# A recommendation kernel with 1.1 million gathered rows: transposes in four PSUM banks, attention as columns, shrinking lags, and another split of the row queues

## The chip, the cores and the metric

The kernel runs on one core of a Trainium2 chip. The metric is the time of the device in microseconds (us), as the median of several runs; smaller is better. The core has five engines that work in parallel, each through its own queue in order: TensorE (PE, matmuls), VectorE (DVE), ScalarE (ACT), GpSimd (POOL) and SyncE (SP). GpSimd, ScalarE and SyncE can each issue DMAs.

## The reference

For each of 16,384 users there are 69 item ids and one label id. Each id picks a row of 96 floats from a table `emb` of 100,001 rows. What is computed, in float32:

```
u  = emb[batch_user]                    # 16384 x 69 x 96
ql = emb[batch_label]                   # 16384 x 96
z  = [ql, u, ql - u, ql * u]            # 384 wide
h  = dice(z @ W1 + b1)                  # 64 wide
att = (h @ W2 + b2) @ W3 + b3           # one number for each user and item
pre = u * att  where id < 100000, else 0
pooled = window @ pre                   # 69 items summed into 10 groups
x  = [pooled, ql]                       # 11 * 96 wide
x  = dice(x @ Wf1 + bf1); x = dice(x @ Wf2 + bf2)      # 200, then 80 wide
out = x @ Wf3 + bf3
dice(x) = (a * (1 - p) + p) * x,  p = sigmoid(x)
```

## The kernel before

The users are cut into 32 blocks of 512. Within a block the items are cut into 69 chunks of 512 rows: 64 chunks hold 8 users with their first 64 items each ("main"), 5 hold one of the last items of all 512 users ("tail"). A step `i` takes two chunks, so there are 1104 steps (`NPAIR`). A chunk is four tiles of 128 rows, one row per partition.

**Getting rows.** Most tiles are fetched by GpSimd with one indirect DMA of 128 rows (`gather`, L268) into a buffer `u` of the step; 17 such buffers take turns. One tile in some of the chunks (`SLOT`) is fetched otherwise: SyncE or ScalarE issues 128 DMAs of one row each (class `Singles`, L303) into one of the buffers of `ring`, four for SyncE and three for ScalarE. `SP_CHUNKS` and `ACT_CHUNKS` list these chunks. SyncE has a tile every 10 steps. ScalarE has a tile every 8 steps and issues 16 rows of it in each step, between its activations (`ACT_ROWS`). For each group of rows the offsets are loaded into registers first (L288).

**The work of a step**, in the order of the data:

- `fetch` (L361): TensorE transposes the eight tiles, four to a PSUM bank `ptr` (pool `ps_tr`, two banks); VectorE copies it to `uT` (L378) and multiplies it with the label's row to `quT` (L381).
- `hidden` (L391): TensorE makes the first layer of both chunks in one bank `ph` (L401, L405), ScalarE the sigmoid `y` (L407). `product` (L411): two VectorE operations make dice out of it.
- `attend_rows` (L417): for four steps together, TensorE makes the attention numbers as rows of a bank `prow` (L421), ScalarE copies them to `row` (L423). `turn_band` (L433): TensorE transposes `row` into `patt` (L438), so that the numbers stand one to a partition. `weigh` (L443): VectorE makes of `patt` the weights `rw` of the ten groups (L448).
- `pool_sums` (L460): eight matmuls of 20 columns of `u` with `rw` into a set of `acc` (three sets), `pool_copy` (L482): VectorE copies it to `pooled`. After `pool_sums` the buffer `u` is free for a gather 17 steps on.
- Tail chunks: `attend_tail` (L426) makes the attention over all partitions (`pa`) and VectorE the product `pre` (L431).
- For each block, once: `head_gather`, `head_turn` and `head_rows` prepare the label's rows, and `top1` to `top3` (L508 to L541) make the last three layers. The last block's top is made in four quarters of 128 users.

PSUM has eight banks here: two `ps_tr`, two `ps_h`, two `ps_x` (prow, patt, pa, pq, pc), one `acc`, one `ps_m` (the top).

**The order** is written out by hand: a dictionary `plan` gives each step its list of work, and every engine carries out its part in that order (`at`, L631). Lags keep the stages apart: in step `i` the transposes are those of `i`, `hidden` that of `i - 2`, `product` that of `i - 3`, `pool_sums` that of `i - 9` (`POOL_LAG`). Near the end, from step `c - 8` on with `c = NPAIR - 8`, another list is written out, with smaller lags. The last tail chunks of a block are its last five; in the last block they are moved forward (`EARLY`, `chunk_of`).

Of the kernel before, what the change touches and what calls it, by code (L numbers as in the profile page):

```python
# [18 lines left out]
P = 128  # L19
# [21 lines left out]
POOL_LAG = 9  # L41
# [5 lines left out]
CLOSE = 8  # L47

# [3 lines left out]
SP_CHUNKS = [2 * (10 * s + 8) + 1 for s in range(109)]  # L52
SP_RING = 4
ACT_CHUNKS = [2 * (8 * s + 11) for s in range(136)]
ACT_RING = 3
ACT_ROWS = 16
# [6 lines left out]

def chunk_of(c):

    n, k = divmod(c, NCH)
    if n == NBLK - 1 and k >= EARLY:
        k = NMAIN + k - EARLY if k < EARLY + NTAIL else k - NTAIL
    return n, k
# [47 lines left out]
def rec_kernel(  # L117
# [132 lines left out]
    ps_tr = ctx.enter_context(tc.tile_pool(name="ps_tr", bufs=2, space=PSUM))  # L250
    ps_h = ctx.enter_context(tc.tile_pool(name="ps_h", bufs=2, space=PSUM))
    ps_x = ctx.enter_context(tc.tile_pool(name="ps_x", bufs=2, space=PSUM))
    ps_acc = ctx.enter_context(tc.tile_pool(name="ps_acc", bufs=1, space=PSUM))
    acc = ps_acc.tile([E, 3, 2, NS, G], F32, tag="acc", name="acc")
    ps_m = ctx.enter_context(tc.tile_pool(name="ps_m", bufs=1, space=PSUM))


# [86 lines left out]
    def head_rows(n):  # L344

        for h in range(2):
            pc = ps_x.tile([P, NMAIN // 8, H1], F32, tag="x", name=f"pc{n}_{h}")
            for k in range(NMAIN // 8):
                x = (h * NMAIN // 8 + k) * 4 * NS
                nc.tensor.matmul(pc[E:P, k, :], qTs[n % 2][:, x : x + 4 * NS], Cq, start=True, stop=True)  # L350
            nc.scalar.copy(As[n % 2][E:P, h * NMAIN // 8 : (h + 1) * NMAIN // 8, :], pc[E:P])
# [65 lines left out]
    def attend_rows(b, n):  # L417

        pr = ps_x.tile([P, 512], F32, tag="x", name=f"prow{b}")[0 : 32 * n]
        for k in range(n):  # L420
            nc.tensor.matmul(pr[32 * k : 32 * (k + 1), :], v2, ys[b + k], start=True, stop=True)  # L421
        row = rpool.tile([P, 512], F32, tag="row", name=f"row{b}")[0 : 32 * n]
        nc.scalar.copy(row, pr)  # L423
        bands[b] = row
# [8 lines left out]
    def turn_band(b, n):  # L433

        row = bands.pop(b)
        pt = ps_x.tile([P, 4, n, 32], F32, tag="x", name=f"patt{b}")
        for t in range(4):
            nc.tensor.transpose(  # L438
                pt[:, t].rearrange("p k j -> p (k j)"), row[:, t * P : (t + 1) * P], ident[0 : 32 * n, 0 : 32 * n]
            )  # L440
        turned[b] = pt

    def weigh(b, n):  # L443

        pt = turned.pop(b)
        rw = rpool.tile([P, 16, 2, 2 * G], F32, tag="rw", name=f"rw{b}")[:, 0 : 4 * n]
        for j in range(2):
            nc.vector.scalar_tensor_tensor(  # L448
                rw[:, :, j, :],
                pt.rearrange("p t k j -> p (t k) j")[:, :, j : j + 1].to_broadcast([P, 4 * n, 2 * G]),  # L450
                bb,
                R.rearrange("p (o g) -> p o g", o=1).to_broadcast([P, 4 * n, 2 * G]),
                ALU.add,
                ALU.mult,
            )
        for k in range(n):
            rws[b + k] = rw[:, k::n]
            ys.pop(b + k)

    def pool_sums(i):  # L460

        u, rw = us.pop(i), rws.pop(i)
        todo = [(j, *chunk_of(2 * i + j)) for j in range(2)]
        todo = [(j, n, k) for j, n, k in todo if k < NMAIN]
        if not todo:
            return
        pa = acc[:, i % 3]
        for j, n, k in todo:
            for t in range(4):
                read_rows(  # L470
                    nc.tensor.matmul,
                    pa[:, j, 2 * t : 2 * t + 2, :].rearrange("e n g -> e (n g)"),
                    u,
                    2 * i + j,
                    t,
                    rw[:, t, j, :],
                    start=True,
                    stop=True,
                )
        accs[i] = pa, todo  # L480
# [27 lines left out]
    def top1(n, cols, h, part, p1):  # L508

        if part == 0:  # L510

            banks, tag = (ps_h, "h") if n == NBLK - 1 and cols.start >= BLK // 2 and h == 1 else (ps_m, "m")
            p1 = banks.tile([DH, BLK], F32, tag=tag, name=f"p1_{n}_{h}_{cols.start}")[:, cols]
# [13 lines left out]
    def top2(n, cols):  # L527
        x2 = xpool.tile([D2, BLK], F32, tag="x2", name=f"x2_{n}_{cols.start}")[:, cols]
        g2 = xpool.tile([DH, BLK], F32, tag="g1", name=f"g2_{n}_{cols.start}")[0:D2, cols]
        p2 = ps_m.tile([D2, BLK], F32, tag="m", name=f"p2_{n}_{cols.start}")[:, cols]  # L530
# [5 lines left out]
    def top3(n, cols, x2):  # L536
        k0, k1 = cols.start // P, cols.stop // P
        p3 = ps_m.tile([P, k1 - k0], F32, tag="m", name=f"p3_{n}_{cols.start}")
# [4 lines left out]
    def store(n):  # L543

        p4 = ps_x.tile([n, P], F32, tag="x", name="p4")
# [5 lines left out]
    def top3_last(x2):  # L551

        p3 = ps_m.tile([1, P], F32, tag="m", name="p3_last")
# [5 lines left out]
    pooled, pres, x1s, x2s, qs, us, hs, ys, bands, rws, p1s, gates, turned, accs = ({} for _ in range(14))  # L559

    def top_steps(n, cols):


        def half(h, part):
            if n not in x1s:
                x1s[n] = xpool.tile([DH, 2, BLK], F32, tag="x1", name=f"x1_{n}")
            p1s[n] = top1(n, cols, h, part, p1s.get(n))
# [9 lines left out]
    def rows_of(b, n):  # L577
        return lambda: attend_rows(b, n)

    def spread_of(b, n):  # L580
        def work():
            turn_band(b, n)
            weigh(b, n)

        return work
# [72 lines left out]
    e = c - CLOSE  # L658
    for i in range(e):
        if i >= 7 and i % 4 == 3 and i < e - 1:  # L660
            at(i, rows_of(i - 7, 4))
        if i >= 4:
            at(i, tails_of(i - 4))
        if i >= 8 and i % 4 == 0:
            at(i, lambda b=i - 8: turn_band(b, 4))
# [3 lines left out]
        pools = [] if i < POOL_LAG else [i - POOL_LAG]  # L669
        if i == e - 2:  # L670
            pools.append(i - POOL_LAG + 1)
        elif i == e - 1:
            pools = [i - POOL_LAG + 1]
        at(i, *[lambda k=k: pool_sums(k) for k in pools])
        if i >= 3:
            at(i, product_of(i - 3))
        at(i, *[lambda k=k: pool_copy(k) for k in ([] if i <= POOL_LAG else [i - POOL_LAG - 1, i - POOL_LAG][: 1 + (i == e - 1)])])
        if i == e - 2:
            at(i, rows_of(c - 16, 4))
        elif i == e - 1:  # L680
            at(i, lambda: turn_band(c - 16, 4))
        at(i, fetch_of(i))
        if i >= 8 and i % 4 == 0:
            at(i, lambda b=i - 8: weigh(b, 4))
        elif i == e - 1:
            at(i, lambda: weigh(c - 16, 4))

    at(e, product_of(e - 3), lambda: pool_copy(e - POOL_LAG), tails_of(e - 4))
    for i in range(e, c):
        if (i - 3) % 4 == 3:  # L690
            at(i, rows_of(i - 6, 4))
        at(i, tails_of(i - 3))
        if (i - 4) % 4 == 3:
            at(i, spread_of(i - 7, 4))
        at(i, hidden_of(i - 2), lambda i=i: scalar_rows(i))
        for k in {0: (-16, -15), 1: (-14,), 2: (-13,), 3: (-12, -11), 4: (-10, -9), 7: (-8, -7)}.get(i - e, ()):
            at(i, pool_of(c + k))
        at(i, fetch_of(i))

    at(c, pool_of(c - 6), pool_of(c - 5), tails_of(c - 3), hidden_of(c - 2), fetch_of(c))  # L700
    at(c + 1, tails_of(c - 2), hidden_of(c - 1), fetch_of(c + 1))
    at(c + 2, rows_of(c - 4, 4), tails_of(c - 1), hidden_of(c), spread_of(c - 4, 4), pool_of(c - 4), fetch_of(c + 2))
    at(c + 3, pool_of(c - 3), pool_of(c - 2), hidden_of(c + 1), fetch_of(c + 3, [hidden_of(c + 2)]))
    at(c + 4, pool_of(c - 1), fetch_of(c + 4, [hidden_of(c + 3)]))
    at(c + 5, rows_of(c, 4), spread_of(c, 4), pool_of(c), fetch_of(c + 5, [hidden_of(c + 4)]))
    at(c + 6, pool_of(c + 1), pool_of(c + 2), fetch_of(c + 6, [hidden_of(c + 5)]))
    at(c + 7, pool_of(c + 3), rows_of(c + 4, 2), fetch_of(c + 7, [spread_of(c + 4, 2), hidden_of(c + 6)]))

    for n in range(NBLK):
        first, end = n * NCH // 2, ((n + 1) * NCH - 1) // 2  # L710
        if n > 0:
            if n % NIDS == 1:
                at(max(0, first - 50), lambda n=n: load_ids(n))
            at(first - 14, lambda n=n: qs.__setitem__(n, head_gather(n)))
            at(first - 11, lambda n=n: head_turn(n, qs.pop(n)))
            at(first - 9, lambda n=n: head_rows(n))
        if n < NBLK - 2:
            for s, work in enumerate(top_steps(n, slice(0, BLK))):
                at(end + POOL_LAG + 4 + s, work)
        elif n == NBLK - 2:  # L720
            for s, work in enumerate(top_steps(n, slice(0, BLK))):
                at(end + POOL_LAG + 1 + s // 2, work)
# [3 lines left out]
    quarter = [top_steps(NBLK - 1, slice(r * P, (r + 1) * P)) for r in range(NQ)]  # L726
    for s, step in enumerate([1, 1, 1, 2, 2, 2, 2, 3, 3, 3]):
        at(c - 8 + step, quarter[0][s])
    for s, step in enumerate([5, 5, 5, 5, 6, 6, 6, 6, 7, 9]):
        at(c - 8 + step, quarter[1][s])  # L730

    d = NPAIR
    at(d, pool_of(c + 4), hidden_of(c + 7), pool_of(c + 5), *quarter[2][0:4], rows_of(c + 6, 2), quarter[2][4])
    at(d, spread_of(c + 6, 2), *quarter[2][5:8], pool_of(c + 6), quarter[2][8], pool_of(c + 7))
    at(d, quarter[2][9], quarter[3][0], lambda: store(B // P - 1), *quarter[3][1:])
# [79 lines left out]
```

## Time and profile before

| | |
|---|---|
| median of 3 runs | 10,930.59 us (10,930.19 to 10,933.84) |
| profiled execution, its own time | 13,684.32 us |
| its span, first to last instruction | 13,682.6 us |
| mean granted TensorE clock | 0.72 |
| busy: TensorE, VectorE, ScalarE, GpSimd | 9,106, 5,075, 991, 8,225 us |
| gathers by GpSimd | 8,587 of items, 128 of labels |
| row DMAs by SyncE, ScalarE | 13,952, 17,408 |

The profile is of one execution, and that one took a quarter longer than the runs. A row of its groups names a line of the kernel, the engine, what is written and read, the count, the busy time in us, the mean of one in ns, and the idle time of that engine just before, with what ended most of it. A matmul in float32 has two records, a transpose one. DMAs of single rows are not counted as busy.

### The profile page before, as it was taken

What the parts mean: (1) busy time and instruction counts of PE and PEld (TensorE: products, weight loads), DVE (VectorE), ACT (ScalarE), POOL (GpSimd) and SP (SyncE); (2) the same over time, 40 slices, a digit from 0 to 9 for tenths busy, and PEclk for the clock granted to TensorE, in tenths of its full rate; (3) what the DMA queues carried; (4) which work ended last, traced back from release to release, by engine and by line L of the source; (5) the groups of instructions that cost most, each with busy time, mean ns of one, the idle gap of its engine ahead of it and who ended that gap; (6) DMA issues with size and microseconds to landing.
All of it is one profiled execution on the core that took longest, in us unless ns stands there. A gap on an engine that the chain in (4) does not pass through costs nothing.

```text
span 13682.6 us, 171148 instructions
## 1 busy us (share of the span) xinstructions
PE 9106.3 (67%) x41797; PEld 4711.6 (34%) x41797; DVE 5074.9 (37%) x8639; ACT 990.6 (7%) x1657; POOL 8225.3 (60%) x8721
## 2 busy tenths in 40 slices
PE   3666666666666666666776666666666666676668
PEld 1333333333333333333333333333333333333334
DVE  2333333333333333333333333333333333333333
ACT  0000000000000000000000000000000000000001
POOL 5666566656666656666665665665665666556663
PEclk7677776777767777677776777777777777777677
DMA  1111111111111111111111111111111111111111
GB/s 38 34 34 33 34 33 33 33 35 33 33 34 34 35 33 33 33 33 36 33 33 33 33 36 33 34 33 33 36 33 33 34 33 35 33 33 34 33 33 22
DMA packets 344459, 458.45 MB, mean 34 GB/s; under 512 B 202354, under 2 KB 202866, under 8 KB 343330
## 3 DMA queue, kind: packets, MB, share of 16 engines
q0 software_dynamic: 278880, 428.92, 15.0%
q1 hardware_dynamic: 29762, 11.82, 0.4%
q10 hardware_dynamic: 34816, 6.75, 0.3%
q8 instruction: 336, 5.51, 0.2%
q14 instruction: 665, 5.45, 0.1%
HBM read 446.74 MB, written 0.07 MB: 33 GB/s over the span
## 4 chain that ended last, share of the span: by engine, by line
PE 37%; issue 20%; another core or an unknown queue 18%; ACTq 12%; DVE 10%; POOL 2%; ACT 1%; DMA 0%; POOLq 0%
ACTq L303 10%; PE acc L327 8%; PE ph L401 6%; PE ptr L327 6%; PE ph L405 5%; PE p L521 5%; DVE uT L378 3%; DVE quT L381 2%; POOL u L268 2%; PE prow L421 2%; DVE y L415 1%; DVE y L414 1%; ACTq L288 1%; PE pa L430 1%
## 5 line engine op out<-in xcount | busy, mean ns | idle before, releaser
L268 POOL DMA_INDIRECT u<-in_rows,ids x8587 | 8103.5, 944 | 5290.9 <-issue 2228.3
L327 PE MATMUL acc<-rw,u 128*96 128x20 f32 x15930 | 1972.9, 269 | 1685.7 <-issue 1088.5
L489 DVE COPY pooled<-acc 96x160 f32<-96x160 f32 x1008 | 429.0, 426 | 6575.4 <-remote 4728.2
L327 PEld LDWEIGHTS acc<-rw,u 128*96 128x96 f32 x15930 | 1853.6, 201 | 2757.0 <-issue 1954.3
L327 PE MATMUL ptr<-ident,u 128*96 128x128 f32 x8587 | 1655.6, 341 | 866.1 <-issue 659.3
L378 DVE COPY uT<-ptr 96x512 f32<-96x512 f32 x2208 | 1485.9, 673 | 996.2 <-remote 756.4
L405 PE MATMUL ph<-quT,wn 96*64 96x512 f32 x4416 | 1625.1, 727 | 195.2 <-issue 189.6
L401 PE MATMUL ph<-uT,A 128*64 128x512 f32 x4096 | 1637.7, 830 | 156.9 <-issue 106.2
L327 PEld LDWEIGHTS ptr<-ident,u 128*96 128x96 f32 x8587 | 1250.6, 166 | 1082.2 <-issue 864.1
L381 DVE TENSOR_TENSOR quT<-ptr,qT 96x512 f32<-96x512 f32 x2048 | 1378.6, 673 | 0.0
L407 ACT ACTIVATE y<-ph 128x512 f32<-128x512 f32 x1104 | 658.6, 597 | 8853.1 <-remote 3304.5
L405 PEld LDWEIGHTS ph<-quT,wn 96*64 96x64 f32 x4416 | 447.3, 175 | 1257.0 <-issue 1255.2
L414 DVE SCALAR_TENSOR_TENSOR y<-y,na1c,ph 128x512 f32<-128x512 f32 x1104 | 810.3, 734 | 177.1 <-ACT y L407 97.0
L415 DVE SCALAR_TENSOR_TENSOR y<-ph,wn,y 128x512 f32<-128x512 f32 x1104 | 828.8, 751 | 39.4
L521 PE MATMUL p<-pooled,wf 96*100 96x512 f32 (+1 forms) x1400 | 713.8, 643 | 84.9 <-issue 82.0
L438 PE MATMUL patt<-ident,row 128*128 128x128 f32 x1108 | 259.5, 375 | 641.4 <-issue 274.9
L421 PE MATMUL prow<-y,v 128*32 128x512 f32 x2208 | 540.7, 851 | 115.0 <-issue 95.6
L401 PEld LDWEIGHTS ph<-uT,A 128*64 128x64 f32 x4096 | 279.0, 169 | 868.9 <-issue 783.3
L521 PE MATMUL p<-pre,V 96*100 96x512 f32 (+1 forms) x700 | 424.0, 745 | 140.4 <-issue 89.2
L438 PEld LDWEIGHTS patt<-ident,row 128*128 128x128 f32 x1108 | 185.1, 194 | 775.8 <-issue 554.0
L521 PEld LDWEIGHTS p<-pooled,wf 96*100 96x100 f32 x1400 | 251.0, 192 | 450.3 <-issue 450.0
L430 PE MATMUL pa<-y,vrep 64*96 64x512 f32 x320 | 231.3, 895 | 203.2 <-DVE pre L431 127.6
(72 smaller groups left out, 2682.1 us busy)
## 6 DMA issues: line engine op xcount, KB each, us to landing
ring<-in_rows ACTq DMA_DIRECT2D x17408, 0.4 KB
ring<-in_rows SPq DMA_DIRECT2D x13952, 0.4 KB
u<-in_rows,ids POOLq DMA_INDIRECT x8587
ids<-in_idx SPq DMA_DIRECT2D x8, 560.0 KB, 2.5
q<-in_emb,ids POOLq DMA_INDIRECT x128
wf<-in_far SPq DMA_DIRECT2D x1, 1209.0 KB
wn<-in_near SPq DMA_DIRECT2D x1, 236.0 KB, 3.1
ids<-in_idx SPq DMA_DIRECT2D x1, 140.0 KB
```

What stands on the lines that cost most here:

```text
L268: nc.gpsimd.indirect_dma_start(out=dst, out_offset=None, in_=table, in_offset=bass.IndirectOffsetOnAxis(ap=index, axis=0),)
L303: d = self.engine.dma_start(out=ring[r : r + 1, b], in_=row_bytes[:, bass.ds(self.values[r], ROW_BYTES)]).then_inc(self.sems[k], 16)
L327: ins = op(out, ring[:, at[0]].bitcast(F32) if at else u[:, 4 * (c % 2) + t, :], other, **how)
L378: nc.vector.tensor_copy(uT[j][0:E], ptr)
L381: nc.vector.tensor_tensor(quT[:, j, :].rearrange("e (s f) -> e s f", f=FM), ptr.rearrange("e (s f) -> e s f", f=FM), by_field(q[:, k * NS ...
L401: nc.tensor.matmul(p, As[n % 2][:, k // 4, :], uT[j], start=True, stop=False)
L405: nc.tensor.matmul(p, Wp, quT[:, j, :], start=False, stop=True)
L407: nc.scalar.activation(y, ph, AF.Sigmoid, scale=S_DICE)
L414: nc.vector.scalar_tensor_tensor(y, y, na1c, ph, ALU.mult, ALU.mult)
L415: nc.vector.scalar_tensor_tensor(y, ph, a1c, y, ALU.mult, ALU.add)
L421: nc.tensor.matmul(pr[32 * k : 32 * (k + 1), :], v2, ys[b + k], start=True, stop=True)
L521: nc.tensor.matmul(p1, w[:, h * DH : (h + 1) * DH], x, start=(k == 0), stop=(k == KTOP - 1))
```

## The change

- **PSUM.** `ps_tr` has four banks, `ps_x` one. `ps_m` is gone: the top uses `ps_x`, and `ps_tr` for the last block's second half. One bank `shared` holds two sets of sums (columns 0 to 319), five places for attention numbers (320 to 479) and the last layer (from 480).
- **Attention as columns.** `attend_rows` and `turn_band` are gone. `attend` makes four matmuls per step with a 128 x 128 part of `y` as the loaded operand and two columns of `v2` as the moving one, so that the numbers come out one to a partition, in their place of `shared`; `weigh` reads them there.
- **Row queues.** SyncE has 136 tiles, one every 8 steps, ScalarE 98, one every 11 steps, with 12 rows per step. These are 234 tiles instead of 245; the rest stays with GpSimd.
- **Order.** `POOL_LAG` is 10; over the last 48 steps the lag of `pool_sums` goes down to 7 step by step, and attention bands go from four steps to two. In the last 12 and the last 8 steps the lags are smaller still. The quarters of the last block's top have a table `QUARTERS`. In the other blocks the tail chunks are spread (`TAIL_AT`: chunks 48, 53, 58, 63, 68), `head_rows` is made in two parts, and the steps of the top come at `end + 12` to `end + 20`.

```diff
-POOL_LAG = 9
+POOL_LAG = 10
...
+QUARTERS = [
+    [-12, -12, -11, -11, -10, -10, -9, -9, -8, -7],
+    [-5, -5, -5, -4, -3, -3, -3, -2, -1, 0],
+    [3, 3, 3, 4, 5, 5, 5, 6, 7],
+]
...
-SP_CHUNKS = [2 * (10 * s + 8) + 1 for s in range(109)]
+SP_CHUNKS = [2 * (8 * s + 8) + 1 for s in range(136)]
...
-ACT_CHUNKS = [2 * (8 * s + 11) for s in range(136)]
+ACT_CHUNKS = [2 * (11 * s + 14) for s in range(98)]
...
-ACT_ROWS = 16
+ACT_ROWS = 12
...
+TAIL_AT = [48 + 5 * f for f in range(NTAIL)]
...
-    ps_tr = ctx.enter_context(tc.tile_pool(name="ps_tr", bufs=2, space=PSUM))
+    ps_tr = ctx.enter_context(tc.tile_pool(name="ps_tr", bufs=4, space=PSUM))
...
-    ps_x = ctx.enter_context(tc.tile_pool(name="ps_x", bufs=2, space=PSUM))
+    ps_x = ctx.enter_context(tc.tile_pool(name="ps_x", bufs=1, space=PSUM))
...
-    acc = ps_acc.tile([E, 3, 2, NS, G], F32, tag="acc", name="acc")
-    ps_m = ctx.enter_context(tc.tile_pool(name="ps_m", bufs=1, space=PSUM))
+    shared = ps_acc.tile([P, 512], F32, tag="shared", name="shared")
+    sets = shared[0:E, 0:320].rearrange("e (k j s g) -> e k j s g", k=2, j=2, g=G)
+
+    def place(b, n):
+
+        start = 320 + 32 * (b // 4 % 5) + 8 * (b % 4)
+        return shared[:, start : start + 8 * n].rearrange("p (t k j) -> p t k j", t=4, j=2)
...
-    def attend_rows(b, n):
-
-        pr = ps_x.tile([P, 512], F32, tag="x", name=f"prow{b}")[0 : 32 * n]
-        for k in range(n):
-            nc.tensor.matmul(pr[32 * k : 32 * (k + 1), :], v2, ys[b + k], start=True, stop=True)
-        row = rpool.tile([P, 512], F32, tag="row", name=f"row{b}")[0 : 32 * n]
-        nc.scalar.copy(row, pr)
-        bands[b] = row
+    def attend(i, b, n):
+
+        out = place(b, n)
+        for t in range(4):
+            nc.tensor.matmul(out[:, t, i - b, :], ys[i][:, t * P : (t + 1) * P], v2[:, 0:2], start=True, stop=True)
...
-        pa = acc[:, i % 3]
+        pa = sets[:, i % 2]
...
+        for k in [i - 5] if i < f else [i - 5, i - 4] if i == f else [i - 4]:
+            if k >= 0:
+                at(i, lambda k=k: attend(k, k - k % 4, 4) if k < f - 8 else attend(k, k - k % 2, 2))
...
+        pools = range(pooled_to, max(pooled_to, i - (POOL_LAG if i < f else max(7, POOL_LAG - 1 - (i - f) // 6)) + 1))
...
-    at(d, pool_of(c + 4), hidden_of(c + 7), pool_of(c + 5), *quarter[2][0:4], rows_of(c + 6, 2), quarter[2][4])
-    at(d, spread_of(c + 6, 2), *quarter[2][5:8], pool_of(c + 6), quarter[2][8], pool_of(c + 7))
-    at(d, quarter[2][9], quarter[3][0], lambda: store(B // P - 1), *quarter[3][1:])
+    at(d, pool_of(c + 4), hidden_of(c + 7), pool_of(c + 5), quarter[2][9], last[0], rows_of(c + 6, 2))
+    at(d, last[4], lambda: store(B // P - 1), spread_of(c + 6, 2), pool_of(c + 6), pool_of(c + 7))
+    at(d, *last[1:4], *last[5:])
```

## The prediction

> **What bounds the kernel now.** I read the page's busy shares first, then the costliest groups, then GpSimd's timeline in the middle of the run, then the last 130 us.
>
> The page's part 1, and from its part 5 the group of the gathers (busy and mean ns of one, then idle time before them):
>
> ```profile
> PE 9106.3 (67%) x41797; PEld 4711.6 (34%) x41797; DVE 5074.9 (37%) x8639; ACT 990.6 (7%) x1657; POOL 8225.3 (60%) x8721
> L268 POOL DMA_INDIRECT u<-in_rows,ids x8587 | 8103.5, 944 | 5290.9 <-issue 2228.3
> ```
>
> No engine is full in the 13,682.6 us of this span, and that misleads, because the recorded execution is 2,750 us longer than the runs (10,930.59 us). GpSimd's timeline (start, length, idle before it and its releaser) shows why:
>
> ```profile
> 6017.33 0.94 POOL L268 DMA_INDIRECT u<-in_rows,ids  x1 [0.30 <-issue]
> 6018.58 0.95 POOL L268 DMA_INDIRECT u<-in_rows,ids  x1 [0.30 <-issue]
> ...
> 6029.82 0.94 POOL L268 DMA_INDIRECT u<-in_rows,ids  x1 [0.30 <-issue]
> 6031.07 0.94 POOL L268 DMA_INDIRECT u<-in_rows,ids  x1 [0.30 <-issue]
> 6035.76 0.94 POOL L268 DMA_INDIRECT u<-in_rows,ids  x1 [3.76 <-PE ph L405]
> ```
>
> From 6017.33 to 6031.07 lie eleven gathers: **1.249 us from start to start**, 0.944 busy and 0.305 between. The next one waits for a u buffer. There are 8587 + 128 = 8715 gathers. The mean of all undisturbed spacings in the trace is 1.2487, and 8714 of them are 10,881 us, just under the time of the runs. Of the 5,291 us idle, 8587 x 0.305 = 2,619 is this pace; the other 2,672 us are waits for TensorE. First gather at 3.27, 8714 paces, those waits, and 126 us from the last gather's start (13556.61) to the end give the span; its own time is 1.7 us more, 13,684.32. In the runs there is no room for the 2,672 us. They come with the recording: sixteen row DMAs of ScalarE take 5 us in places and 14 in others, and matmuls stretch with them.
>
> ```profile
> 13395.26 13.86 ACTq L303 DMA_DIRECT2D ring<-in_rows  x16
> 13449.49 5.00 ACTq L303 DMA_DIRECT2D ring<-in_rows  x16
> ```
>
> So I take the runs as paced by GpSimd: 10,881 us of paces and 49.4 us for both ends. Three runs within 3.7 us agree: a count of equal gathers repeats so well.
>
> The 49.4 us: 3.3 to the first gather, about 2.6 from the last gather's start to its landing (at the start, the gather at 14.97 is transposed at 17.66), 1.7 outside the span, and the work after the last transposes. That part can be read at the end of the timeline, first and last line of it:
>
> ```profile
> 13648.10 0.64 PE L327 MATMUL ptr<-ident,u 128*96 128x128 f32 x4
> ...
> 13675.98 0.38 PE L532 MATMUL p<-x,wf 100*80 100x128 f32 x2
> ...
> 13680.31 0.24 SPq L557 DMA_DIRECT2D out<-r  x1
> ```
>
> From 13648.10 to 13682.6 are 34.5 us. The sum is 42.1, and 7.3 us remain: TensorE a little behind when the last gather lands, or at its slow clock.
>
> **What the skill says.** The Trainium skill, "Perfetto Trace Analysis", section GPSIMD Engine Instruction, says to time GpSimd by the spacing of starts and not by the reported span; the trace agrees, 1.249 spacing against 0.944 reported. "DMA: Bandwidth & Descriptors", section SWDGE vs HWDGE vs iDMA: software on GpSimd computes the descriptors of its DMAs, and those of SyncE and ScalarE are made by hardware. The trace agrees in that the gather's pace is the same whatever the other queues do. "TensorE: Matmul & The Clock Gate", Part 1: the clock is halved by default and released by sustained activity. Here the mean is 0.72 over the span and 0.80 in the last 123 us, where TensorE is 88% busy: a busier TensorE is a faster one.
>
> **The change part by part.**
>
> *Rows.* SyncE fetches 136 tiles instead of 109, ScalarE 98 instead of 136: 234 instead of 245. Eleven tiles go back to GpSimd, 8726 gathers, all on the path: **11 x 1.249 = +13.7 us**. ScalarE issues 4,864 DMAs fewer (12 per step, not 16), SyncE 3,456 more. SyncE now has eight steps per tile, 8 x 9.86 = 78.9 us, 0.617 us per row (a step is 10,881/1104 = 9.86). In the trace 64 rows at 198.00 took 25.48 us, 0.40 per row with their offset loads, thus 51 us per tile. ScalarE issues 0.31 per row. Both queues together issue 29,952 rows instead of 31,360. I cost this at nothing, hidden behind GpSimd; without that cover SyncE ends the step, see the rivals.
>
> *Attention as columns.* It removes these two groups and the 277 copies of `row` on ScalarE (0.585 each, 162 us, off the path):
>
> ```profile
> L438 PE MATMUL patt<-ident,row 128*128 128x128 f32 x1108 | 259.5, 375 | 641.4 <-issue 274.9
> L421 PE MATMUL prow<-y,v 128*32 128x512 f32 x2208 | 540.7, 851 | 115.0 <-issue 95.6
> ```
>
> That is 800 us of TensorE. It adds 4 x 1104 = 4416 matmuls of two columns, two records each. The nearest rows: acc, 1972.9/15930 = 0.124 us per record, and the one-column p of L540, 49.6/254 = 0.195. So 1,095 to 1,722 us, **TensorE +0.3 to +0.8 us per step**. It is busy 9106/1104 = 8.25 us of a step now, 8.5 to 9.1 then, below 9.86: nothing on the path. Should the cover go, it is worth up to 0.8 x 1104.
>
> *Buffers.* Four banks for transposes take away waits like ptr for DVE (60 us in the recording); two acc sets instead of three, and one ps_x bank for p1, pa, pc and pq, add some. An acc wait of DVE (77 us now) has behind it on TensorE that step's transposes, and DVE and then ScalarE wait for those. With POOL_LAG 10, GpSimd may lead by 17 - 10 = 7 steps, 69 us, instead of 8. A wait shorter than that never reaches it: between 0 and, if TensorE stays behind for good, the rival below. I take 0. Spread tail chunks, split head_rows and later top steps move work between steps and change no count; nothing, under the same lead. The extra gathers use the same queue.
>
> *The end.* After the last transposes the old order has both halves of quarter 2's top, quarter 3 whole, `row`, its turn and the store between. The new one has, by the old rows: transposes 0.35, two DVE passes 1.3, hidden 0.6, sigmoid 0.6, product 1.5, attention columns 1.0 to 1.6, weigh 0.7, two pool_sums 3.0, pool_copy 0.4, two halves of quarter 3 at 2.35 (their first parts done earlier) plus 0.5, ten hand-overs of 0.1, and 6.4 from 13676.2 to the end as before: 22.3 us. **34.5 - 22.3 = -12.2 us.** What is late next is the pooled sum before the last top. Of the unexplained 7.3 us the lags that shrink over 48 steps may take all or none; I take half, -3.6.
>
> Sum: 10,930.6 + 13.7 - 12.2 - 3.6 = 10,928.5; I say **10,929 us**. Against the recorded execution the same terms stand, +13.7 and -12.2 on 13,684, but its waits of 2,672 us may move by more than that.
>
> **Rivals.**
>
> *TensorE becomes the bound.* For it: 8.5 to 9.1 us busy in 9.86, waits not counted, one ps_x bank. Against: the clock rises with load, and the lead is 69 us. It decides from 9.86 us per step; at 10.1 it costs 0.24 x 1104 = 265: 11,190 us. Slower.
>
> *SyncE's rows become the bound.* It decides above 0.617 us per row. The runs of before prove only 10,930/13,952 = 0.783. At 0.65: 136 x 128 x 0.65 = 11,315 us. For: the mean in the recording is 0.94 (13,174 us from its first row to its last). Against: 0.40 where it is undisturbed.
>
> *The pace is itself stretched by the recording.* If it is 1.24 in the runs, before has some 76 us of waits for TensorE in it, and the new buffers could return most: 10,850 us. Against: the intervals do not vary while all other queues do.
>
> *The end doesn't get shorter*, because TensorE is late there: 10,944 us.
>
> **How the numbers follow.** A measurement of this kernel can tell about 0.2% from no change, 22 us. The likeliest case, and the unshortened end, lie within it: 0.65, own range 10,917 to 10,945. Stretched pace, faster: 0.19. TensorE 0.09, SyncE 0.05, unknown stalls 0.02, slower: 0.16. The range 10,870 to 10,990 takes half of the fast cases and the small slow ones, and leaves out some 2 in 10.
>
> **What would show it.** Right: 8598 + 128 gathers at 944 ns and 0.30 between; prow, patt and row gone; a group of 8832 records writing shared; about 22 us from the last transposes to the end. Wrong: a pace other than 1.249; SyncE rows back to back without rest and GpSimd waiting for TensorE that waits for sp; more than 36 us, or under 18, after the last transposes. Below 10,908 us the pace assumption falls; above 10,953 a new bound exists.

## The result, and the profile after

The changed kernel takes 11,003.8 us (median of four runs, 10,997.7 to 11,018.2) against 10,932.1 for the kernel before: **1.0069 times as long, with a 95% interval of 1.0056 to 1.0081, some 72 us slower**. The prediction said 10,929, with 10,870 to 10,990 as its range. It was wrong.

The profiled execution has a span of 10,996.0 us and a time of its own of 10,997.74, so it is one like the runs. Part 1 of the page and the group of the gathers (busy us and mean ns of one, then idle time before them and its releaser):

```profile
PE 10025.2 (91%) x47313; PEld 5972.6 (54%) x47313; DVE 5222.6 (47%) x8725; ACT 848.2 (8%) x1380; POOL 8238.2 (75%) x8732
L287 POOL DMA_INDIRECT u<-in_rows,ids x8598 | 8116.6, 944 | 2623.1 <-issue 2419.3
```

TensorE's share is what catches the eye: 91%. GpSimd's timeline in the middle of the run (start, length, idle before):

```profile
6017.61 0.94 POOL L287 DMA_INDIRECT u<-in_rows,ids  x1 [0.30 <-issue]
6018.86 0.94 POOL L287 DMA_INDIRECT u<-in_rows,ids  x1 [0.30 <-issue]
...
6031.34 0.95 POOL L287 DMA_INDIRECT u<-in_rows,ids  x1 [0.30 <-issue]
```

From 6017.61 to 6031.34 are eleven gathers again, 1.248 us each. Over the whole trace the mean is 1.2490, and only two of 8725 spacings are over 1.4 us. So GpSimd never waits for anybody here: the pace of the prediction holds, and with 11 gathers more it costs 13.7 us. The rest must lie after the last gather. The end of the timeline, of GpSimd, then of TensorE, then of SyncE:

```profile
10901.68 0.94 POOL L287 DMA_INDIRECT u<-in_rows,ids  x1 [0.30 <-issue]
```
```profile
10956.93 0.60 PE L346 MATMUL ptr<-ident,u 128*96 128x128 f32 x4
...
10968.81 3.41 PE L440 MATMUL shared<-v,y 128*128 128x2 f32 x16
...
10992.92 0.38 PE L560 MATMUL p_last<-x,wf 80*1 80x128 f32 x2 [1.36 <-DVE x L510]
```
```profile
10993.70 0.24 SPq L563 DMA_DIRECT2D out<-r  x1
```

The last gather starts at 10,901.68, and its row is there some 2.6 us later, if it lands as the gather that the prediction timed. The last transposes come at 10,957: **TensorE is 53 us behind**. After them 38.7 us pass to the end at 10,996.0. The sum from the last gather's start is 94.3 us. In the order of before with the same gathers (experiment a4) it is 37.1: there the last gather starts at 10,902.22 and the span ends at 10,939.3. So 94.3 - 37.1 = 57.2 us, and with the 13.7 us of the eleven gathers 70.9 of the 72 us are found. The experiments ask what makes TensorE late.

### The profile page after: what moved, and what is told of

It reads as the page before. It is cut to its first block, busy times and chain, and to the rows that moved or that the text cites. A ratio compares the mean times of both kernels' runs of the same rounds, so it can differ in the third digit from the quotient of the medians.

```text
span 10996.0 us, 179100 instructions
## 1 busy us (share of the span) xinstructions
PE 10025.2 (91%) x47313; PEld 5972.6 (54%) x47313; DVE 5222.6 (47%) x8725; ACT 848.2 (8%) x1380; POOL 8238.2 (75%) x8732
## 4 chain that ended last, share of the span: by engine, by line
PE 68%; POOL 12%; DVE 10%; issue 6%; DMA 3%; ACT 1%; POOLq 0%; ACTq 0%
PE shared L346 15%; POOL u L287 12%; PE ptr L346 11%; PE p L527 10%; PE ph L420 9%; PE ph L424 8%; PE shared L440 7%; DMA u<-in_rows,ids 3%; DVE pooled L495 3%; PE pa L446 2%; PE ph L417 2%; DVE uT L397 2%; PE ph L422 2%; DVE y L434 1%; DVE y L433 1%
## 5 line engine op out<-in xcount | busy, mean ns | idle before, releaser
L346 PE MATMUL shared<-rw,u 128*96 128x20 f32 x15954 | 2004.4, 273 | 668.0 <-DVE pooled L495 594.9
L346 PEld LDWEIGHTS shared<-rw,u 128*96 128x96 f32 x15954 | 1881.1, 205 | 763.8 <-DVE pooled L495 674.9
L346 PE MATMUL ptr<-ident,u 128*96 128x128 f32 x8598 | 1929.5, 386 | 228.7 <-DMA u<-in_rows,ids 226.9
L440 PEld LDWEIGHTS shared<-v,y 128*128 128x128 f32 x8832 | 1214.6, 213 | 1228.0 <-issue 961.4
L420 PE MATMUL ph<-uT,A 128*64 128x512 f32 x4096 | 1879.2, 940 | 0.2
L424 PE MATMUL ph<-quT,wn 96*64 96x512 f32 x4416 | 1725.5, 788 | 0.0
L346 PEld LDWEIGHTS ptr<-ident,u 128*96 128x96 f32 x8598 | 1468.2, 187 | 399.3 <-DMA u<-in_rows,ids 336.8
L440 PE MATMUL shared<-v,y 128*128 128x2 f32 x8832 | 1307.3, 270 | 31.5 <-DVE rw L454 26.4
L495 DVE COPY pooled<-shared 96x160 f32<-96x160 f32 x946 | 396.4, 419 | 1635.4 <-PE shared L440 1601.0
L434 DVE SCALAR_TENSOR_TENSOR y<-ph,wn,y 128x512 f32<-128x512 f32 x1104 | 828.8, 751 | 39.4
L446 PE MATMUL pa<-y,vrep 64*96 64x512 f32 x320 | 312.9, 1079 | 2.5 <-DVE pre L447 2.5
```

Source lines behind the costliest of these rows:

```text
L346: ins = op(out, ring[:, at[0]].bitcast(F32) if at else u[:, 4 * (c % 2) + t, :], other, **how)
L420: nc.tensor.matmul(p, As[n % 2][:, k // 4, :], uT[j], start=True, stop=False)
L424: nc.tensor.matmul(p, Wp, quT[:, j, :], start=False, stop=True)
L434: nc.vector.scalar_tensor_tensor(y, ph, a1c, y, ALU.mult, ALU.add)
L440: nc.tensor.matmul(out[:, t, i - b, :], ys[i][:, t * P : (t + 1) * P], v2[:, 0:2], start=True, stop=True)
L495: nc.vector.tensor_copy(pooled[n][:, :, k * NS : (k + 2) * NS].rearrange("e g s -> e s g"), pa.rearrange("e j s g -> e (j s) g"),)
```

## The experiments

Theory 1: GpSimd paces all but the end, and the columns take from TensorE the room that it needs to work off a backlog which builds up in the last 30 steps. Rivals: the new order of the end makes the backlog whatever the form of attention; the banks make it; the new split of the rows makes it.

### a1 to a4: each part by itself

a1 is the changed kernel with the rows split as before:

```diff
-SP_CHUNKS = [2 * (8 * s + 8) + 1 for s in range(136)]
+SP_CHUNKS = [2 * (10 * s + 8) + 1 for s in range(109)]
-ACT_CHUNKS = [2 * (11 * s + 14) for s in range(98)]
+ACT_CHUNKS = [2 * (8 * s + 11) for s in range(136)]
-ACT_ROWS = 12
+ACT_ROWS = 16
```

> The changed kernel with the rows split as before (109 chunks by SyncE, 136 by ScalarE, 16 per step), so 11 gathers fewer; all else as changed. Theory 1 (the steps are paced by GpSimd at 1.249 us per gather, and the rest of the loss is TensorE being late at the end): 11,003.8 - 13.7 = 10,990, within 10 us. Rival (the new split of the rows is what makes TensorE or the rows late): most of the 72 us comes back, about 10,940.

a2 is the changed kernel with attention as rows: `attend_rows` and `turn_band` of before are back, called in the step of a band's last `attend` and just ahead of `weigh`. To make room it has three banks for transposes instead of four, and one of its own for the top.

```diff
-    ps_tr = ctx.enter_context(tc.tile_pool(name="ps_tr", bufs=4, space=PSUM))
+    ps_tr = ctx.enter_context(tc.tile_pool(name="ps_tr", bufs=3, space=PSUM))
+    ps_m = ctx.enter_context(tc.tile_pool(name="ps_m", bufs=1, space=PSUM))
...
-            nc.tensor.matmul(out[:, t, i - b, :], ys[i][:, t * P : (t + 1) * P], v2[:, 0:2], start=True, stop=True)
+            nc.tensor.matmul(pr[32 * k : 32 * (k + 1), :], v2, ys[b + k], start=True, stop=True)
...
-        pt = place(b, n)
+        pt = turned.pop(b)
```

> The changed kernel with the attention as rows again (one 512-wide matmul per pair, a copy by ScalarE, four turns per band), at the changed kernel's places in the steps; to make room, three banks for transposes instead of four and one bank of its own for the top. Schedule, lags, end and rows as changed. Theory 1 (the columns' 8832 small matmuls take the room that TensorE needs to catch up at the end): the lateness at the end goes, about 10,945 (13.7 us of it over the kernel before are the 11 gathers). Rival A (the new order of the end and the shrinking lags make TensorE late, with rows as with columns): stays at 10,990 to 11,005.

a3 has both edits, and a4 is the kernel before with the three lines of the new split alone.

> Both of the above: attention as rows and the rows of the table split as before, on the changed schedule. Theory 1: 10,930, or down to 10,917 if the new order of the end is worth the 12 us that the prediction gave it. Rival A (the end order itself is late): 10,975 to 10,990.

> The kernel before with only the new split of the rows (136 chunks by SyncE, 98 by ScalarE, 12 per step; 11 more gathers). Theory 1: 10,932 + 13.7 = 10,945. Rival B (SyncE's rows cannot keep up with a chunk every 8 steps, and hold up the transposes): over 10,960.

Measured, against 10,931.6 for the kernel before on the same chip (the first row against 10,932.1, as above):

| kernel | us | ratio to before | lag at steps 1076, 1084, 1092, 1103 |
|---|---|---|---|
| changed | 11,003.8 | 1.0069 (1.0056 to 1.0081) | 3, 45, 58, 53 |
| a1, old split | 11,000.9 | 1.0067 (1.0053 to 1.0081) | 3, 48, 73, 68 |
| a2, rows | 10,947.7 | 1.0015 (1.0008 to 1.0022) | 0, 37, 29, 14 |
| a3, rows and old split | 10,954.4 | 1.0022 (1.0013 to 1.0031) | 0, 34, 42, 31 |
| a4, before with new split | 10,944.5 | 1.0011 (1.0005 to 1.0018) | 0, 17, 10, 0 |

The lag (in us) is worked out from each trace: the start of a step's last transpose, less the start of the last gather of the rows up to that step, less 2.6 us for its landing. Step 1103 is the last one.

Three terms follow. The new split alone costs 10,944.5 - 10,931.6 = 12.9 us, as 11 gathers should (13.7). The order, lags and banks with attention as rows add 3.2 (a2 less a4). The columns, with the banks that go with them, add 56.1 (changed less a2); f3 below tells the two apart.

The lags show the shape. **The new order, with its lags and its two sets of sums, doubles the backlog, and the columns keep it.** Between steps 1076 and 1084 the top of block 30, the last block's tail chunks, the first parts of its own top and the work that smaller lags bring forward come together. In a4 the lag rises to 17, in a2 to 37. Then a2 takes back 23 us in 19 steps, and the changed kernel takes back none. Busy time by stretch, cut at the last transposes of steps 1040, 1076, 1084 and 1103; the columns are the stretch, its length, busy us (and instructions) of PE, PEld, DVE, ACT and POOL, the granted clock, the share of the DMAs and GB/s. First the changed kernel:

```profile
10286.40:10641.40 355.00, 326.28 (x1575) 198.00 (x1573) 171.03 (x296) 27.14 (x44) 268.38 (x285) 0.72 0.20 42
10641.40:10760.50 119.10, 107.73 (x433) 57.81 (x432) 45.86 (x81) 9.87 (x15) 89.92 (x96) 0.75 0.19 40
10760.50:10957.30 196.80, 177.25 (x987) 125.62 (x985) 89.36 (x162) 18.79 (x37) 107.59 (x114) 0.72 0.14 30
```

a2, attention as rows:

```profile
10282.20:10637.90 355.70, 286.41 (x1410) 143.29 (x1408) 170.21 (x296) 35.23 (x59) 268.82 (x285) 0.77 0.17 41
10637.90:10752.60 114.70, 105.27 (x412) 47.95 (x413) 45.02 (x79) 12.19 (x19) 86.81 (x92) 0.78 0.17 40
10752.60:10917.70 165.10, 150.72 (x895) 93.28 (x893) 89.16 (x162) 24.56 (x47) 113.28 (x120) 0.84 0.15 37
```

a4, the order of before:

```profile
10284.20:10638.70 354.50, 285.21 (x1337) 135.29 (x1335) 170.52 (x278) 32.20 (x53) 268.00 (x284) 0.74 0.17 41
10638.70:10733.20 94.50, 82.80 (x348) 37.16 (x349) 39.07 (x64) 10.34 (x16) 71.54 (x76) 0.84 0.17 40
10733.20:10904.80 171.60, 147.46 (x871) 92.29 (x870) 95.49 (x166) 20.61 (x38) 128.53 (x137) 0.81 0.17 40
```

In the first stretch all three take 355 us for 36 steps, GpSimd's pace of 9.86 us each. But TensorE is busy 326 of it as columns (9.06 us a step) and 286 as rows (7.96). In the second, eight steps take 119 and 115 us in the new order and 94.5 in the old: 432 and 412 records against 348, since more of the last block's work and more pool sums lie there. In the third, 19 steps take 165 us with rows, 8.7 a step, which is catching up, and 197 with columns, 10.4 a step.

What makes these 32 us can be read from the same rows. 5 us are TensorE's pauses, 26.5 its busy time. Of that the attention itself is 8.5: 27.5 us (176 records) as columns, 14.2 and 4.8 (84 records) as rows and their turns. The other 18 us are work that both kernels have: 811 records, which take 149.8 us at the clock of 0.72 and 131.8 us at 0.84. So the columns keep the backlog more by the lower clock that goes with them than by their own time.

What becomes of the slack is in TensorE's own waits (us in all, times, longest). The changed kernel, a2 and a4, two waits of each:

```profile
PE shared L346 <- DVE pooled L495: 594.9, 927, 2.1
PE ptr L346 <- DMA u<-in_rows,ids: 226.9, 291, 2.0
```
```profile
PE ptr L347 <- DMA u<-in_rows,ids: 1322.4, 1541, 2.2
PE shared L347 <- DVE pooled L509: 614.0, 413, 4.2
```
```profile
PE ptr L327 <- DMA u<-in_rows,ids: 1917.6, 2234, 3.5
...
PE acc L327 <- DVE pooled L489: 6.3, 6, 1.9
```

A wait for the gather's row is TensorE's free time. It is 1,918 us in the order of before, 1,322 in the new one with rows, 227 with columns. The first loss, 596 us, is about what TensorE waits in a2 for `pool_copy` to empty one of the two sets of sums, 614 us; with three sets, in a4, that wait is 6.3 us.

The miss of these four is a1 (10,990 was expected) and with it a3 (10,930): eleven gathers fewer gain 3 us in one, and a3 is 6.7 us slower than a2. Where TensorE is late at the end, an earlier last gather moves nothing. And the old split makes TensorE later still, by a path that the chain of waits of a1 shows (start, length, what):

```profile
10760.48 1.73 PE ph L424 x4
10762.23 0.60 ACT y L426
10762.83 1.61 ACTq L307
...
10769.63 0.21 ACTq L322
10769.94 0.38 ACT g L508
10770.34 0.50 ACT g L509
10770.87 0.35 DVE x L510
10771.22 0.60 DVE uT L397
10771.86 2.31 PE ph L420 x3
```

ScalarE loads offsets and issues 16 row DMAs between the sigmoid and the gate `g` of the top: 7.1 us, and nearly as much once more from 10,788. VectorE's `uT` copy is queued behind the `x` that needs `g`, and TensorE behind `uT`. With the old split ScalarE issues rows up to step 1088, with the new one up to step 1078, before the last block's top begins (step 1084).

### b1 to b4, c1 to c4, d1 and d2: the question could not be seen

These ten runs were to tell the banks from the columns, and the last steps from the rest. They fell on three chips on which the kernel before itself takes 13,523, 13,641 and 13,628 us. Of the five chips used here two run the kernel before in 10,932 us and three in over 13,500.

b1 is the changed kernel with the banks of a2 (three for transposes, one for the top). b2 makes columns up to step 1048 and rows after, b3 rows and then columns, by a condition on the band in a2's functions:

```diff
+    def columns(b):
+        return b >= NPAIR - CLOSE - 48      # b3; with < in b2
```

b4 is the kernel before with `SP_CHUNKS` of 136 tiles, one every 8 steps, beside its 136 of ScalarE. c1, c2 and c3 are b2, b3 and b4 again, d1 is b3 once more. c4 and d2 are the kernel before with `attend`, in a bank of its own, in the place of `attend_rows`, and with one `ps_x` bank:

```diff
-            nc.tensor.matmul(pr[32 * k : 32 * (k + 1), :], v2, ys[b + k], start=True, stop=True)
+            attend(b + k, b, n)
```

> The changed kernel, attention as columns, with the banks of the kernel with attention as rows: three for transposes and one of its own for the top. Theory 1 (the attention's form made the difference between 11,003.8 and 10,947.7, not the banks): 11,000 to 11,008. Rival (the top in ps_x, or the fourth bank, made it): 10,945 to 10,980.

> Attention as columns in all steps up to 56 before the last 8 (step 1048), as rows from there; three banks for transposes, the rest as changed. Theory 1 (the columns cost time only where TensorE has a backlog that it must work off, in the last 30 steps): about 10,950, as with rows throughout. Rival (columns cost in all steps, by a backlog that is carried through the run): 10,985 to 11,000.

> The other way round: attention as rows up to step 1048, as columns in the last 56 steps. Theory 1: 10,985 to 11,003, as with columns throughout. Rival: about 10,955.

> The kernel before with 136 tiles by SyncE (one every 8 steps) and 136 by ScalarE as it was: 272 instead of 245, so 27 gathers fewer. Theory 1 (in the kernel before GpSimd's pace sets the time, with TensorE caught up at the end): 10,931.6 - 27 x 1.249 = 10,898. Rival (fewer gathers leave TensorE late at the end, as with the changed kernel's order): 10,915 to 10,932.

> The kernel of b2 once more (columns up to step 1048, then rows), since that run fell on a chip on which the kernel before takes 13,523 us and its question is about a chip on which it takes 10,932 us. There, theory 1 (columns cost time only where TensorE has a backlog to work off, in the last 30 steps): about 10,950. Rival (a backlog carried through the whole run): 10,985 to 11,000. On a chip as in b2: 14,300 again, since there TensorE's columns are on the path all through (0.44 us per step between b2 and b3).

> The kernel of b3 once more (rows up to step 1048, then columns). Where the kernel before takes 10,932 us, theory 1: 10,985 to 11,003; it differs from the kernel with rows throughout (10,947.7, same banks) only in the last 56 steps. Rival: about 10,955. On a chip as in b3: 13,830.

> The kernel of b4 once more (the kernel before with 272 tiles by SyncE and ScalarE, 27 gathers fewer). Where the kernel before takes 10,932 us, theory 1: 10,898 (27 x 1.249 less). Rival (TensorE late at the end): 10,915 to 10,932. On a chip as in b4: 13,680.

> The kernel before, its order, lags and rows, with attention as columns alone (four matmuls per pair into a bank of their own, made where the rows were made; one ps_x bank). Theory 1: columns add some 1 us of TensorE to a step, and the crowd of the last 30 steps adds lateness whatever the order: 10,932 + 20 to 50 = 10,950 to 10,980. Rival (only together with the new order of the end do columns cost anything): 10,925 to 10,940. On a chip where the kernel before takes 13,523: over 13,900.

> Attention as rows up to step 1048, as columns in the last 56 steps, banks as in the kernel with rows throughout (10,947.7). Where the kernel before takes 10,932 us: theory 1 (columns cost time where TensorE has a backlog to work off, in the last 30 steps, whatever the banks) 10,985 to 11,003; rival (the banks, or a backlog carried through the run) about 10,950. Where it takes over 13,500 us, 1.022 times the kernel before, as twice already.

> The kernel before, its order, lags and rows, with attention as columns alone. Where the kernel before takes 10,932 us: theory 1 (the crowd of the last 30 steps adds lateness whatever the order) 10,950 to 10,980; rival (columns cost only together with the new order of the end) 10,925 to 10,940. Where it takes over 13,500 us, 1.045 times the kernel before, as once already.

| kernel | us (before on the same chip) | ratio |
|---|---|---|
| b1, columns, banks of a2 | 14,334.9 (13,522.7) | 1.0588 (1.0564 to 1.0612) |
| b2, columns, then rows | 14,296.6 (13,522.7) | 1.0570 (1.0553 to 1.0587) |
| c1, the same | 14,578.7 (13,640.7) | 1.0697 (1.0672 to 1.0721) |
| b3, rows, then columns | 13,833.6 (13,522.7) | 1.0225 (1.0207 to 1.0244) |
| c2, the same | 13,934.4 (13,640.7) | 1.0219 (1.0198 to 1.0239) |
| d1, the same | 13,944.3 (13,628.0) | 1.0234 (1.0211 to 1.0256) |
| b4, 136 and 136 tiles | 13,679.7 (13,522.7) | 1.0109 (1.0091 to 1.0126) |
| c3, the same | 13,908.2 (13,640.7) | 1.0198 (1.0179 to 1.0217) |
| c4, before with columns | 14,252.3 (13,640.7) | 1.0446 (1.0427 to 1.0464) |
| d2, the same | 14,230.0 (13,628.0) | 1.0437 (1.0420 to 1.0454) |

They tell nothing on the end, but they do tell what those chips are like. ScalarE's timeline in b4, and in the changed kernel's trace for comparison:

```profile
7001.27 10.59 ACTq L303 DMA_DIRECT2D ring<-in_rows  x16
```
```profile
5001.08 3.56 ACTq L322 DMA_DIRECT2D ring<-in_rows  x12
```

Sixteen rows take 10.59 us, 0.66 each, against 0.30 each. In c3 the chain of waits has turned into SyncE's rows:

```profile
SPq 56%; issue 40%; PE 3%; DVE 0%; another core or an unknown queue 0%; ACTq 0%; POOL 0%; ACT 0%; DMA 0%; POOLq 0%
```

On such a chip a row costs SyncE up to 13,908 / 17,408 = 0.80 us, 27 gathers fewer with 27 more tiles for SyncE make the kernel slower, not faster (b4 and c3), and there is no free time to hide columns in: b2, with columns in the first 1048 steps, is 463 us slower than b3, with columns in the last 56. Why rows are slow there no run tells.

### f1 to f4: the same questions without single rows

To be free of that, all four have one tile by SyncE and one by ScalarE, and GpSimd gathers the rest:

```diff
-SP_CHUNKS = [2 * (10 * s + 8) + 1 for s in range(109)]
+SP_CHUNKS = [2 * (10 * s + 8) + 1 for s in range(1)]
-ACT_CHUNKS = [2 * (8 * s + 11) for s in range(136)]
+ACT_CHUNKS = [2 * (8 * s + 11) for s in range(1)]
```

f1 is the kernel before so changed, f2 the changed kernel, f3 the kernel of b3, f4 that of c4.

> The kernel before with one tile each by SyncE and ScalarE instead of 109 and 136; GpSimd gathers the rest. Theory 1 (steps are paced by GpSimd; chips where it takes over 13,500 us are slow only in the issue of single rows): 8958 gathers, 8957 x 1.249 = 11,187, and 42 us of both ends (3.3 to the first gather, 37.1 from the last one's start to the end, 1.7 outside the span): 11,229 on any chip. Rival (those chips are slow in TensorE or in the gathers): well over 11,229 there, 13,000 and more.

> The changed kernel with one tile each by SyncE and ScalarE. Theory 1: the same 8958 gathers, and 94 us from the last gather's start to the end as in its trace, less some 3 us since a step is 0.13 us longer: 11,283, that is 54 us over f1. If the split of the rows had made the loss, it is level with f1.

> As f2, with attention as rows up to step 1048 and as columns in the last 56 steps, three banks for transposes and one of its own for the top. Theory 1 (columns cost time only in the crowd of the last 30 steps, whatever the banks): within 10 us of f2. Rival (banks, or a backlog carried through the run): within 10 us of f1.

> As f1, with attention as columns alone, in the order of before. Theory 1 in its broad form (the crowd of the last 30 steps makes TensorE late whatever the order): 10 to 45 us over f1. Rival (columns cost only together with the new order of the end): within 5 us of f1.

They ran on a chip where the kernel before takes 10,932.4 us. So what f1 was to say on the other kind of chip stays open; the rest came out:

| kernel | us | over f1 | lag at steps 1076, 1084, 1092, 1103 |
|---|---|---|---|
| f1, before | 11,229.7 (11,227.8 to 11,237.0) | | 0, 16, 11, 0 |
| f2, changed | 11,285.8 (11,282.2 to 11,300.3) | 56.1 | 5, 49, 62, 64 |
| f3, columns in the last 56 steps only | 11,282.3 (11,277.5 to 11,288.2) | 52.6 | 0, 42, 51, 46 |
| f4, before with columns | 11,253.8 (11,247.1 to 11,264.2) | 24.1 | 0, 24, 23, 20 |

(The lags are those of the profiled execution, which takes 11,237.0 us in f1, 11,300.3 in f2, 11,277.5 in f3 and 11,247.1 in f4.)

f1 lands within a microsecond of 8957 paces and two ends (8957 x 1.249 + 42.1 = 11,229.4). f3 has the banks of a2, and rows in the first 1048 steps, and is still within 3.5 us of f2. **So columns in the last 56 steps are enough for the whole loss**; the changed banks aren't needed for it, and what columns do to the other 1048 steps is hidden. That rows throughout take the loss away was run only with the row queues, in a2, which is 3.2 us over a4. f4 says the order is not needed for a loss, but doubles it: 24 us in the old order, some 53 in the new. (f4 has one `ps_x` bank instead of two, but so has a2.) The lag of f4 rises from 0 to 24 in the crowd, against 16 in f1, and then stays, as in the changed kernel.

Not tried: whether three sets of sums, or the last block's top begun a few steps later, would let the columns pay; and no run parts the columns' own time from the clock. No version faster than both kernels came out; on the two chips of the prediction's question, 136 and 136 tiles in the order of before was not seen.

## Why the prediction was wrong, point by point

- **The pace: right.** 1.249 us per gather is measured with no GpSimd wait to speak of, and f1 comes out from it to within 1 us. But its reason was wrong. The prediction put the 2,672 us of GpSimd's waits in the profile of before down to the recording. In a4 the profiled execution takes 10,941.1, and the runs lie from 10,940.0 to 10,948.8. The profile of before looks like those of the three other chips: 13.86 us for 16 rows of ScalarE (in b4 13.76 for 15), and a span of 13,682.6 where the kernel before takes 13,502 to 13,656 there. I take it to be of such a chip. Nor are the 2,672 us all waits for TensorE: of GpSimd's idle time ahead of gathers the profile puts 1,059 us down to the transposes, and 1,517 us to another core or an unknown queue.
- **Rows, +13.7: right by itself** (12.9 in a4). In the changed kernel the term is void, as a1 shows.
- **Columns, "+0.3 to +0.8 us per step ... nothing on the path": this is the step that failed.** First its size. The rows that answer to prow and patt, the groups of the changed kernel and then those of a2:

```profile
L440 PE MATMUL shared<-v,y 128*128 128x2 f32 x8832 | 1307.3, 270 | 31.5 <-DVE rw L454 26.4
L440 PEld LDWEIGHTS shared<-v,y 128*128 128x128 f32 x8832 | 1214.6, 213 | 1228.0 <-issue 961.4
```
```profile
L458 PE MATMUL patt<-ident,row 128*128 128x128 f32 (+1 forms) x1156 | 265.6, 377 | 2.4 <-DVE rw L468 2.4
```

  The columns' 1,307 us, 0.148 per record, are within the estimate of 1,095 to 1,722. But prow (364.5) and patt took 630 us, not 800: the 800 were read from a profile of the other kind of chip. And TensorE's busy time rose by 10,025.2 - 8,815.4 (a2) = 1,210 us, 533 more than 1,307 - 630. The same other work took longer where the mean clock was 0.708 instead of 0.753; the pool sums alone went from 1,796 to 2,004 us. The prediction had said that a busier TensorE is a faster one, from the Trainium skill, "TensorE: Matmul & The Clock Gate", section "Part 1: The HAM clock gate", by which activity releases the throttle. Here a TensorE busy 91% of the time had a lower clock than one busy 80%; the trace disagrees with my use of the page. So it was +1.10 us per step: 0.61 for the attention, inside the predicted range, and 0.48 for the other work, which the prediction had at nothing. Second, the cover. An average of 9.06 of 9.86 us, in the first stretch above, did fit, and columns in the first 1048 steps cost no more than 3.5 us (f2 less f3). In the last 30 steps the crowd needs more than the pace gives and there is no later to put it off to. The cover was the slack after the crowd, and there the columns and the lower clock had spent it. That is 56 us (changed less a2).
- **Buffers, 0: right for GpSimd, not for TensorE.** Two sets of sums cost TensorE 595 us of waits. No gather waited, but it is the same slack.
- **The end, 34.5 to 22.3: wrong.** It is 38.7 us, in a2 35.0, and in the order of before 34.6 (a4) to 39.4 (f1). The new order does leave less for the end, 161 records on TensorE against 221. But they run slower. The first and the second half of the end in the changed kernel and in a4, with the granted clock third from the right:

```profile
10957.26:10975.00 17.74, 14.55 (x78) 11.58 (x76) 7.24 (x17) 0.92 (x2) 0.00 (x0) 0.68 0.00 0
10975.00:10993.50 18.50, 15.00 (x86) 14.14 (x86) 2.28 (x7) 2.58 (x6) 0.00 (x0) 0.66 0.02 4
```
```profile
10904.75:10922.75 18.00, 18.00 (x151) 15.34 (x151) 6.85 (x15) 3.75 (x8) 0.00 (x0) 0.96 0.01 1
10922.75:10937.00 14.25, 11.09 (x72) 10.10 (x71) 1.93 (x7) 2.58 (x6) 0.00 (x0) 0.74 0.02 6
```

  a4 does 151 records in 18 us at a clock of 0.96 without a pause; the changed kernel does 78 in 17.7 at 0.68, with pauses. The 48 records of the last top (two halves taken at 2.35 each and 0.5) took 8.6 us, sixteen attention records 3.4 instead of 1.0 to 1.6, the two pool sums 6.0 instead of 3.0, the first layer 3.8 instead of 0.6. The term was summed from durations in the last 34.5 us of the profile of before, where the clock was 0.89, and 1.00 in the first half. The 0.6 was too small even so: in a4, at 0.96, the first layer took 2.1. The prediction's own sign that it is wrong, more than 36 us after the last transposes, came.
- **The unexplained 7.3 us, half taken:** the opposite came, 53 us of lateness. A small part of it was the pace: 8714 of 1.2490, as here, are 10,884, where 1.2487, as in the profile of before, gave 10,881.
- **Rivals.** "TensorE becomes the bound" named the right engine with the wrong place: it put the turn at 9.86 us a step over all 1104 steps, and it came in the last 30 alone. "SyncE's rows become the bound" didn't come where the prediction was asked (0.32 us a row, with time to spare), but is what c3 shows on another chip. "The end doesn't get shorter because TensorE is late" had the right mechanism, but let it cost no more than the hoped-for gain: it gave 10,944, and the measured time is 60 us above that. The profile offered the number to ask for: how far behind the gathers TensorE is, step by step, not only how busy it is on average.

## What to carry to other kernels

An engine that is off the path on average can still be on it in the last steps, where what is late cannot be made up. Ask of any work added to it how long its backlog at the end takes to drain: busy time per step against the pacing engine's step, there, not over the run. Price that busy time at the clock that the new work leaves, not at the old one. Work moved ahead of the last load helps only if that engine is idle ahead of it. And look first whether the profile's own time agrees with the runs: if not, it may be of a different chip, and its durations and waits are not those of the runs.

## What the runs showed that was not expected

- Chips differ. On two the kernel before takes 10,932 us with ScalarE's row DMAs 0.30 us apart; on three it takes 13,523 to 13,641, and there many rows take longer (16 in 10.59 us in b4). On those the same edits weigh differently: columns in the order of before cost 4.4% there, against 0.2% between f4 and f1 (24 of 11,230 us, without the single rows).
- TensorE's granted clock went down with more but shorter matmuls, from 0.753 (41,845 records, 80% busy) to 0.708 (47,313 records, 91% busy). The traces show what it goes with. They give the clock in windows of 3.41 us, each at full or at half clock. Add up the moving columns of the matmuls that start in a window (2 for a record of attention as columns, 512 as rows, 128 for a transpose) and look at the clock of the next one. In the changed kernel (3,140 windows, without the run's first 50 and its last ones) none of the 545 that follow one with under 1,000 moving columns is at full clock, though TensorE was busy for 81% of those; after 4,000 and more, 483 of 487 are. In a2 it is 0 of 573 and 869 of 887. The correlation with the next window's clock is 0.75 for the columns in both kernels, and 0.48 and 0.58 for the busy time. So attention as columns keeps TensorE busy and brings few moving columns: 646 per us in the third stretch above, against 921 as rows. This is read from traces; no run varied it by itself.
- At the end of the kernel 78 records took as long as 151 (17.7 and 18.0 us), at clocks of 0.68 and 0.96 and with pauses in the one and none in the other. How much of it is the clock, how much the pauses and how much the kind of records is not shown.
